# An attention kernel's opening, weight products and last transposes put in another order

## The chip, the cores and the metric

One core of one Trainium2 chip runs the whole kernel. The metric is the device time of one execution in microseconds (us); the time of a kernel is the median of several executions. Engines are named as in the profile: PE is the TensorE matmul stream and PEld its weight loads, DVE is VectorE, ACT is ScalarE, POOL is GpSimd, SP is SyncE, whose queue issues all DMAs of this kernel.

## What is computed

Two attention layers follow one another on an image `x` of 8 batches, 32 by 32 positions (N = 1024) and C = 256 channels, all in f32. Layer 0 has 4 heads, layer 1 has one with a narrow key of 32.

```python
# layer 0
qkv = jnp.einsum('bnc,cd->bnd', xf, W_qkv)      # q, k, v of 4 heads, 256 each
atten = softmax(jnp.einsum('bihd,bjhd->bijh', q, k) * C ** -0.5, axis=2)
res = jnp.einsum('bijh,bjhd->bihd', atten, v).reshape(B, -1, h * C)
x = jnp.einsum('bnd,dc->bnc', res, W_out) + b_out + xf
# layer 1
f, g, h = x @ Wf + bf, x @ Wg + bg, x @ Wh + bh
x = gamma * softmax(g @ f.T) @ h + x
```

## The kernel before, in words

**Layer 0 is folded.** A head's scores are `x (Wq Wk^T) x^T` and its output is `softmax(..) x (Wv Wout)`. So the kernel first forms, for each head h, two 256 by 256 products out of the weights: `wqk` and `wvo`. `fold_weights(h)` (L286) returns five tasks for it: `turn_q`, `turn_k`, `turn_v` (L291), each of which makes four 128 by 128 transposes on PE into one PSUM tile (`pwq`, `pwk`, `pwv`, L296) and copies the tile out (`wqT`, `wvT`; L174 on DVE for q and v, L176 on ACT for k); then `multiply` (L307) twice, each with four 128 by 256 matmuls (L312) into `pwqk` or `pwvo` and a copy out (L174 on DVE for `wqk`, followed there by four small additions `wt`, L846; L176 on ACT for `wvo`). An f32 matmul stands in the trace as two PE records, an f32 transpose as one.

**Products in seven parts.** Queries, scores and value products are done by a Strassen-like scheme, `seven` (L227): seven block products instead of eight, in three tasks `one`, `two`, `three`. Task `one` fills three PSUM banks x, y and z, ACT copies x out (`e`, L263) and DVE adds y to it (`u`, L257). Task `two` accumulates into x and y again; DVE then forms `v` (L257) out of y. Task `three` accumulates into y and z a last time, so it must wait until `v` has been read from y. The sums of the blocks of the image that this needs (`xs`, L399 on DVE) come from `key_sums`, those of the value side (`xt`, L415) from `value_sums`.

**PSUM.** The tag `psm` has two tiles (L862). Weight transposes, weight products, image transposes (`px`), layer 1's projections (`pm_fg`) and output projections (`po`) all take turns in these two: the third of them waits for the copy out of the first. The products in seven parts have six tiles of their own, `ps`.

**Order.** PE, DVE and ACT run in exactly the order in which the program issues the tasks (`manual_schedule`). Work is laid out in steps; a step is half of the query rows (`blk`) of one head of one batch, or half of a layer 1. In a step, `put(tasks, *places)` gives each task a place between about 0 and 10 and the tasks are issued in the order of places. In a layer 0 step the scores stand at 0, 2, 4, 6, 8, 10: two groups of `one`, `two`, `three`. The value products of the step before and the output projection of the step before that are put in between.

**Opening.** `load_x(0, 2)` issues four DMAs of 256 KB for the first image, then `load_weights(h, tag)` (L183) issues for each head a DMA of 512 KB for its q and k weights, one of 256 KB for v and one of 256 KB for the output weights; then small constants (`load_rest`, L158). Five matmuls on zeros (`pm_idle`, L873) come first on PE. Then the tasks of the opening run: four image transposes (`transpose_rows`, L336, L344: halves k = 0, 1 by channel blocks c = 0, 1), the three weight transposes of head 0 with a block sum in between, its two products, its queries with two weight transposes of head 1 in the middle, and the sums over the queries. The other 13 tasks of `fold_weights` for heads 1 to 3 are put at fractions 1.5, 2.1, 2.7, ... of step 0.

**Where the weights lie.** The weights of heads 0 and 3 take the two tiles of the tag `s`, which later hold scores; those of head 1 one of the four tiles of `rows` (which otherwise hold images), those of head 2 a tile of `v`.

**End.** The last step (L979 on) belongs to layer 1 of batch 6: its products (`pa_l`, L828) stand at 1, 4, 6, 8 and the last output projections of batch 7 at 3 and 7. At 8.1 to 8.4 come the four transposes of the finished rows of batch 7 (`px`, copied by ACT, L347), at 9 to 9.3 the projections f and g for its layer 1 (`pm_fg`, L440; ACT adds the bias, L667, and DVE copies, L668). Then follow the scores of the last layer 1 (`ps_l`, L740) and its products.

Of the kernel before, what the change touches and what calls it, by code (L numbers as in the profile page):

```python
# [16 lines left out]
P = 128  # L17
# [3 lines left out]
def kernel(  # L21
# [51 lines left out]
    nc = tc.nc  # L73
# [4 lines left out]
    CC = C // P  # L78
# [31 lines left out]
    def tile_of(tag, shape, name):  # L110
        return pools[tag].tile(shape, F32, tag=tag, name=name)
# [4 lines left out]
    def load_x(b, parts=1):  # L116
        t = tile_of("rows", [P, NT, C], f"x_{b}")
        n = HT // parts
        for k in range(NBLK):
            for i in range(parts):  # L120
                nc.sync.dma_start(
                    t[:, k * HT + i * n : k * HT + (i + 1) * n, :].rearrange("p t c -> p (t c)"),
                    x_v[b][:, k, ts(i, n * C)],
                )
        rows[b] = t
# [57 lines left out]
    def load_weights(h, tag):  # L183

        nw = CC * 3 * C
        t = tile_of(tag, [P, nw + CC * C], f"w_{h}")
        w = t[:, :nw].rearrange("p (c d) -> p c d", c=CC)
        wo = t[:, nw:].rearrange("p (c d) -> p c d", c=CC)
        for part in (slice(0, 2 * C), slice(2 * C, 3 * C)):
            nc.sync.dma_start(w[:, :, part], wqkv_v[:, :, ts(h, 3 * C)][:, :, part])  # L190
        nc.sync.dma_start(wo, wout_v[:, ts(h, CC), :])
        weights[h] = w, wo

# [90 lines left out]
    def fold_weights(h):  # L286

        wT, hold = [], []
        folded[h] = []

        def turn(i, what):  # L291
            w, _ = weights[h]
            pt = tile_of("psm", [P, NB], f"pw{what}_{h}")
            for d in range(CC):
                for c in range(CC):
                    nc.tensor.transpose(  # L296
                        pt[:, d * C + c * P : d * C + (c + 1) * P],
                        w[:, c, i * C + d * P : i * C + (d + 1) * P],
                        ident,
                    )  # L300
            if i != 1:
                hold.append(tile_of("y", [P, N], f"w{what}T_{h}"))
            t = hold[-1][:, ts(i % 2, NB)]
            copy_on(i, t, pt)
            wT.append(t.rearrange("p (d c) -> p d c", d=CC))

        def multiply(i, what):  # L307
            wqT, wkT, wvT = wT
            pm = tile_of("psm", [P, NB], f"p{what}_{h}")
            for c in range(CC):  # L310
                for d in range(CC):
                    nc.tensor.matmul(  # L312
                        pm[:, ts(c, C)],
                        lhsT=(wqT, wvT)[i][:, d, ts(c, P)],
                        rhs=wkT[:, d, :] if i == 0 else weights[h][1][:, d, :],
                        start=(d == 0),
                        stop=(d == CC - 1),
                    )
            t = const.tile([P, CC, C], F32, tag=f"{what}{h}", name=f"{what}{h}")
            copy_on(i, t.rearrange("p c e -> p (c e)"), pm)  # L320
            folded[h].append(t)
            if i == 0:
                t4 = const.tile([P, 4, P], F32, tag=f"wt{h}", name=f"wt{h}")
                sums = [t4[:, k, :] for k in range(4)]
                blocks = [t[:, c, ts(e, P)] for c in range(CC) for e in range(CC)]
                run(sum_b(sums, *blocks))
                wblocks[h] = b_operands(blocks, sums)

        tasks = [partial(turn, i, what) for i, what in enumerate(("q", "k", "v"))]
        tasks += [partial(multiply, i, what) for i, what in enumerate(("wqk", "wvo"))]  # L330
        return tasks

# [510 lines left out]
    def run(*lists):  # L843
        for l in lists:
            for t in l:
                t()  # L846

    def weave(*lists):
# [15 lines left out]
    fast.enter_context(tc.manual_schedule(  # L864
        engines={mybir.EngineType.PE, mybir.EngineType.DVE, mybir.EngineType.Activation}
    ))
    load_x(0, 2)
    idle = tile_of("rs", [P, P], "idle")
    nc.vector.memset(idle, 0.0)
    ident = identity()  # L870
    pm = tile_of("psm", [P, NB], "pm_idle")
    for _ in range(5):
        nc.tensor.matmul(pm[:, :P], lhsT=idle, rhs=idle, start=True, stop=True)  # L873
    load_weights(0, "s")
    load_weights(1, "rows")
    load_weights(2, "v")
    load_weights(3, "s")
    load_rest()

    def behind(b):  # L880
# [10 lines left out]

    first = steps[0][0]
    queries, qsums = first.queries()
    turn_q, turn_k, turn_v, *multiply = fold_weights(0)
    sums = key_sums(0)
    run(transpose_rows(0, rows, xT_of, 0), [turn_q, turn_k, sums[0], turn_v], sums[1:3])
    fold = fold_weights(1) + fold_weights(2) + fold_weights(3)
    run(multiply, sums[3:], queries[:2], fold[:2], queries[2:], qsums)
    first_sums = value_sums(0)

    def is_l0(s):
# [8 lines left out]
    for i, (a, blk) in enumerate(steps):  # L910
        l0 = isinstance(a, Layer0)
        one, two, nxt = step(i - 1), step(i - 2), step(i + 1)
        places = []

        def put(tasks, *at):
            assert len(tasks) == len(at)
            places.extend(zip(at, range(len(places), len(places) + len(at)), tasks))

        if l0:
            put(a.scores(blk), 0, 2, 4, 6, 8, 10)  # L920
        else:
            tasks, _ = a.scores(blk)
            put(tasks, *((0.5, 2.4) if blk == 0 else (0.5, 2)))
        if is_l0(two):
            u, k = two
            put(u.products_of[k][2:], 1 if l0 else 0)
            put([partial(u.invert, k)], 2.9 if l0 or blk == 1 else 1.9)
            put(u.project(k), *((3, 7) if l0 else (2, 6) if blk == 0 else (3, 7)))
        if is_l0(one):
            u, k = one  # L930
            sums, keys = u.sums(k)
            u.products_of[k] = u.products(k)
            put(sums[:2] + sums[3:], *((2.2, 3.2, 4.2) if l0 else (0.8, 2.2, 4.5)))
            put(sums[2:3], 5.2 if l0 else 5.5)
            put(keys, *((6.2, 8.2) if l0 else (7.6, 9.6)))
            put(u.products_of[k][:2], *((5, 9) if l0 else (4, 7)))
        elif one is not None:
            put(one[0].products(one[1]), *((3, 5, 7, 9) if l0 else (1, 4, 6, 8)))
        if i == 0:
            put(fold[2:], -2, -1, *[1.5 + 0.6 * n for n in range(len(fold) - 4)])  # L940
            put(first_sums[:2], 8.4, 9.4)
        if i == 1:
            put(first_sums[2:], 1.4, 3.4)
            put([partial(nc.vector.tensor_scalar, bh_sb, bh_sb, gamma_sb, None, ALU.mult)], 8.5)

        if is_l0(nxt) and blk == NBLK - 1:
            queries, qsums = nxt[0].queries()
            put(queries, *((2.5, 4.5, 6.5) if not l0 else
                            (1.5, 2.5, 4.5) if is_l0(two) else (0.5, 2.5, 5.5)))
            put(qsums, *((6.7, 6.9, 7.3, 7.6) if not l0 else  # L950
                          (5.4, 6.4, 7.2, 7.4) if is_l0(two) else (6.4, 7.2, 7.3, 7.4)))

        if l0 and a.h == 0 and blk == 0:
            put(residual(a.b), 5.3, 6.3, 7.3, 7.4)
        if l0 and a.h == 0 and blk == 1 and a.b > 0:
            put(value_sums(a.b), 1.4, 2.4, 3.4, 4.4)
        if l0 and a.h == 2 and blk == 0 and a.b + 1 < B:
            load_x(a.b + 1)
        if l0 and a.h == 2 and blk == 1 and a.b + 1 < B:
            moves, squares = turn_rows(a.b + 1, rows, xT_of, 0)  # L960
            put(moves, *range(1, 9))
        if l0 and a.h == HEADS - 1 and blk == 0 and a.b + 1 < B:
            put(squares, 0.4, 1.4, 3.4, 4.4)
            put(key_sums(a.b + 1), 5.4, 6.4, 7.2, 7.4)

        if l0 and a.b > 0 and a.h == behind(a.b) - 1:
            if blk == 0:
                moves, turned = turn_rows(a.b - 1, rows1, x1T_of, 1, step(i + 2)[0].fg_tile)
                put(moves, 0.1, 0.2, 0.3, 0.4)
                put(turned, 5.4, 6.4, 7.2, 7.4)  # L970
            else:
                tasks, moves = nxt[0].queries_apart()
                put(tasks, 1.5)
                put(moves, 1.6, 1.7, 1.8, 1.9)
        if not l0 and blk == 0:
            put(a.values(), 0.9, 1, 3, 5, 8)
        if nxt is None:
            put(transpose_rows(B - 1, rows1, x1T_of, 1), 8.1, 8.2, 8.3, 8.4)
            put(final.queries(), 9, 9.1, 9.3)  # L979
        for _, _, t in sorted(places, key=lambda x: x[:2]):  # L980
            t()

# [142 lines left out]
```

## Time and profile before

| what | value |
|---|---|
| time, median of 4 runs (lowest to highest) | 2341.54 us (2340.53 to 2341.98) |
| the profiled execution's own time | 2341.12 us |
| its span, from the first to the last instruction | 2339.2 us |
| PE busy | 2328.7 us |
| DVE busy | 1482.5 us |
| ACT busy | 522.8 us |
| POOL busy | 211.6 us |
| DMA, mean over the span | 18 GB/s |

The execution took 1.9 us outside the span. In a row of the profile's timeline the columns are: start in us, length in us, engine, source line, operation, out<-in by the program's names, partitions and elements, number of instructions, and in brackets the idle time of the engine before the row and what ended it. Ends of matmuls are modelled, so what PE lost between two groups is read from start to start: from the first group's start to the next one's, less the number of records times the steady distance between records. That distance in this trace is 0.216 us for 128x256, 0.429 us for 128x512, and 0.108 us for an f32 transpose of 128x128.

### The profile page before, as it was taken

To read this page: it belongs to the slowest core of one execution; us is meant where nothing else is said; L and a number is where in the kernel's file an instruction comes from. 1 tells how busy PE (TensorE), PEld (TensorE's weight loads), DVE (VectorE), ACT (ScalarE), POOL (GpSimd) and SP (SyncE) were. 2 spreads that over 40 slices of the span, in tenths; PEclk is the share of its full clock that TensorE was granted. 3 is DMA by queue.
4 is the path that set the end of the run, shared out by engine and by line. 5 is a ranking of instruction groups with operands and counts; after the bars stand their busy time and mean duration, and the time that the engine had idled before them with its cause. 6 is when DMAs were issued, how large, how long until landed. Compare 5 with 4: busy or idle time off the path is not lost.

```text
span 2339.2 us, 26029 instructions
## 1 busy us (share of the span) xinstructions
PE 2328.7 (100%) x10394; PEld 1917.8 (82%) x10394; DVE 1482.5 (63%) x2398; ACT 522.8 (22%) x875; POOL 211.6 (9%) x79
## 2 busy tenths in 40 slices
PE   9999999999999999999999999999999999999999
PEld 7888888788877888788887888878888788888877
DVE  6667775377754767557774577645776457766635
ACT  2222222222221222212222122222222222212222
POOL 0111110011110111101111011110001101100110
PEclk9999999999999999999999999999999999999999
DMA  5000010100101001110011000110001100000100
GB/s 138 1 1 1 1 37 14 34 1 8 30 17 32 1 19 21 19 29 1 19 26 18 23 1 19 30 19 19 1 19 30 20 17 1 1 1 1 30 10 29
DMA packets 170257, 42.94 MB, mean 18 GB/s; under 512 B 158160, under 2 KB 163024, under 8 KB 170128
## 3 DMA queue, kind: packets, MB, share of 16 engines
q1 hardware_dynamic: 170128, 41.20, 8.1%
q8 instruction: 84, 1.38, 0.3%
q14 instruction: 45, 0.37, 0.1%
HBM read 13.37 MB, written 8.52 MB: 9 GB/s over the span
## 4 chain that ended last, share of the span: by engine, by line
PE 99%; DVE 1%; ACT 0%; DMA 0%; issue 0%; SPq 0%; ACTq 0%
PE psy_y L240 14%; PE psy L240 14%; PE psx L240 10%; PE pa_l L828 9%; PE po L631 9%; PE psx_y L240 9%; PE psz_y L240 9%; PE psz L240 9%; PE psy_q L240 4%; PE psx_q L240 2%; PE psz_q L240 2%; PE pr_v_l L460 2%; PE ps_l L740 1%; PE pm_fg L697 1%; PE pwqk L312 0%; PE pwvo L312 0%
## 5 line engine op out<-in xcount | busy, mean ns | idle before, releaser
L587 POOL PARTITION_ALL_REDUCE rb<-rs x64 | 207.0, 3234 | 2047.5 <-DVE rs L585 2020.7
L240 PE MATMUL psx<-q,x0T 128*128 128x256 f32 x1024 | 263.5, 380 | 0.0
L240 PE MATMUL psy<-qs,xs 128*128 128x256 f32 x1024 | 262.9, 379 | 0.0
L240 PE MATMUL psz<-q,xs 128*128 128x256 f32 x1024 | 262.8, 379 | 0.0
L535 ACT ACTIVATE p<-p 128x1024 f32<-128x1024 f32 x128 | 135.3, 1057 | 561.6 <-DVE p L257 561.6
L240 PE MATMUL psy_y<-s,xt 128*128 128x256 f32 x1024 | 242.4, 380 | 0.1
L631 PE MATMUL po<-wvo,y 128*128 128x256 f32 x1024 | 242.0, 379 | 0.0
L240 PE MATMUL psx_y<-p,x 128*128 128x256 f32 x1024 | 241.9, 379 | 0.0
L828 PE MATMUL pa_l<-v_l,s_l 128*128 128x257 f32 x1024 | 231.9, 381 | 0.4 <-DVE v_l L723 0.4
L240 PEld LDWEIGHTS psx<-q,x0T 128*128 128x128 f32 x1024 | 193.9, 190 | 45.4 <-issue 20.7
L631 PEld LDWEIGHTS po<-wvo,y 128*128 128x128 f32 x1024 | 194.5, 190 | 40.0 <-issue 15.1
L828 PEld LDWEIGHTS pa_l<-v_l,s_l 128*128 128x128 f32 x1024 | 193.7, 190 | 36.8 <-issue 10.5
L240 PEld LDWEIGHTS psx_y<-p,x 128*128 128x128 f32 x1024 | 194.6, 190 | 34.1 <-issue 8.6
L240 PEld LDWEIGHTS psy_y<-s,xt 128*128 128x128 f32 x1024 | 191.7, 190 | 31.2 <-issue 2.7
L240 PEld LDWEIGHTS psy<-qs,xs 128*128 128x128 f32 x1024 | 194.5, 190 | 26.8 <-DVE qs L506 0.4
L240 PEld LDWEIGHTS psz<-q,xs 128*128 128x128 f32 x1024 | 194.6, 190 | 26.4
L257 DVE TENSOR_TENSOR u<-psy,e 128x512 f32<-128x512 f32 x128 | 88.5, 692 | 146.4 <-PE psy L240 72.3
L269 ACT ACTIVATE p<-psx 128x512 f32<-128x512 f32 x128 | 76.4, 597 | 410.3 <-PE psx L240 410.2
L257 DVE TENSOR_TENSOR v<-psy,e 128x512 f32<-128x512 f32 x128 | 87.9, 687 | 125.3 <-PE psy L240 125.3
L240 PE MATMUL psy<-qs,x0T 128*128 128x256 f32 x512 | 131.5, 379 | 0.8 <-DVE v L257 0.8
L642 DVE SCALAR_TENSOR_TENSOR x<-po,inverse,x 128x256 f32<-128x256 f32 x256 | 112.0, 479 | 31.4 <-PE po L631 22.7
L263 ACT COPY e<-psx 128x512 f32<-128x512 f32 x128 | 73.9, 577 | 256.1 <-PE psx L240 256.1
(120 smaller groups left out, 2840.9 us busy)
## 6 DMA issues: line engine op xcount, KB each, us to landing
out_dram<-x SPq DMA_DIRECT2D x15, 512.0 KB, 2.6
x<-in_x_dram SPq DMA_DIRECT2D x14, 512.0 KB, 4.6
x0T<-x SPq DMA_DIRECT2D x224, 32.0 KB, 1.9
fg<-x SPq DMA_DIRECT2D x112, 64.0 KB, 2.1
fg<-fg SPq DMA_DIRECT2D x56, 64.0 KB, 2.0
w<-in_L_conv_W_qkv_dram SPq DMA_DIRECT2D x4, 512.0 KB, 7.4
x<-in_x_dram SPq DMA_DIRECT2D x4, 256.0 KB, 4.0
w<-in_L_conv_W_qkv_dram SPq DMA_DIRECT2D x4, 256.0 KB, 6.8
```

Of the source, the lines that this page charges most:

```text
L240: nc.tensor.matmul(banks[k][:, ts(i, w)], lhsT=lhsT, rhs=rhs, start=first and n == 0, stop=True, skip_group_check=True,)
L257: nc.vector.tensor_tensor(dst, shaped(banks[k]), shaped(other), ALU.add)
L263: nc.scalar.copy(scratch("e"), banks["x"])
L269: copy(outs["11"](), shaped(banks["x"]))
L460: nc.tensor.matmul(pm[:, ts(j, C)], lhsT=src()[:, c, ts(2 * t2 + j, P)], rhs=w()[:, c, :], start=(c == 0), stop=(c == CC - 1),)
L535: exp(both, both)
L587: nc.gpsimd.partition_all_reduce(t, r.rearrange("p e i -> p (e i)"), P, bass_isa.ReduceOp.add)
L631: nc.tensor.matmul(pm[:, ts(j, C)], lhsT=self.y[blk][:, c, ts(2 * t2 + j, P)], rhs=folded[self.h][1][:, c, :], start=(c == 0), stop=(c == ...
L642: nc.vector.scalar_tensor_tensor(acc, pm[:, ts(j, C)], inverse[:, n : n + 1], acc, ALU.mult, ALU.add)
L697: nc.tensor.matmul(pm[ts(k, half)], lhsT=w[:, c, :], rhs=x1T_of[b][:, c, ts(k, NB)], start=(c == 0), stop=(c == CC - 1),)
L740: nc.tensor.matmul(pm, lhsT=self.f[ts(r, CK), ts(j0 + r, P)], rhs=self.g[ts(r, CK), ts(blk, NB)], start=True, stop=True,)
L828: nc.tensor.matmul(pm[:, : C + 1], lhsT=p[:, j, ts(ti, P)], rhs=v[:, j, : C + 1], start=(j == 0), stop=(j == NT - 1),)
```

## The change

- **Opening, DMA.** `load_weights` issues only on request: it returns two tasks, one for q and k and one for v and the output weights. Head 0's q and k weights are issued ahead of the image, its v and output weights behind it.
- **Opening, order of tasks.** The q and k weights of head 0 are transposed first, then half 0 of the image, then the product `wqk`, then half 1 of the image, then the v weights, two block sums, the product `wvo`, the other two block sums, and the queries as before.
- **Tiles.** Head 3's weights take a tile of `rows` instead of `s`.
- **Heads 1 to 3.** Head 1's remaining three tasks and head 2's five are put in step 0 at -2, -1, 0.5, 1.5, 2.5, 4.5, 6.5, 8.5; head 3's five in step 1 at 0.5, 2.6, 3.5, 5.5, 7.5.
- **End.** In the last step the products stand at 1, 4, 7.2, 8.5; the transposes of batch 7 at 2.5, 4.5, 8.1, 8.2; the f and g projections at 2.4 (which only names tiles), 6.5 and 9.
- `multiply` names the transposed weights by their place in a list instead of unpacking the list first.

```diff
         weights[h] = w, wo
+        v = wqkv_v[:, :, ts(h, 3 * C)]
+
+        def load_qk():
+            nc.sync.dma_start(w[:, :, : 2 * C], v[:, :, : 2 * C])
+
+        def load_v():
+            nc.sync.dma_start(w[:, :, 2 * C :], v[:, :, 2 * C :])
+            nc.sync.dma_start(wo, wout_v[:, ts(h, CC), :])
+
+        return [load_qk, load_v]
...
-                        lhsT=(wqT, wvT)[i][:, d, ts(c, P)],
-                        rhs=wkT[:, d, :] if i == 0 else weights[h][1][:, d, :],
+                        lhsT=wT[2 * i][:, d, ts(c, P)],
+                        rhs=wT[1][:, d, :] if i == 0 else weights[h][1][:, d, :],
...
+    load_qk, load_v = load_weights(0, "s")
+    load_qk()
     load_x(0, 2)
+    load_v()
...
-    load_weights(0, "s")
-    load_weights(1, "rows")
-    load_weights(2, "v")
-    load_weights(3, "s")
+    for h, tag in ((1, "rows"), (2, "v"), (3, "rows")):
+        run(load_weights(h, tag))
     load_rest()
...
-    turn_q, turn_k, turn_v, *multiply = fold_weights(0)
-    sums = key_sums(0)
-    run(transpose_rows(0, rows, xT_of, 0), [turn_q, turn_k, sums[0], turn_v], sums[1:3])
-    fold = fold_weights(1) + fold_weights(2) + fold_weights(3)
-    run(multiply, sums[3:], queries[:2], fold[:2], queries[2:], qsums)
+    turn_q, turn_k, turn_v, fold_qk, fold_vo = fold_weights(0)
+    turn_x, sums = transpose_rows(0, rows, xT_of, 0), key_sums(0)
+    fold = [fold_weights(h) for h in range(1, HEADS)]
+    run([turn_q, turn_k], turn_x[:2], [fold_qk], turn_x[2:], [turn_v], sums[:2], [fold_vo])
+    run(sums[2:], queries[:2], fold[0][:2], queries[2:], qsums)
...
-            put(one[0].products(one[1]), *((3, 5, 7, 9) if l0 else (1, 4, 6, 8)))
+            put(one[0].products(one[1]), *((3, 5, 7, 9) if l0 else (1, 4, 6, 8) if nxt else (1, 4, 7.2, 8.5)))
         if i == 0:
-            put(fold[2:], -2, -1, *[1.5 + 0.6 * n for n in range(len(fold) - 4)])
+            put(fold[0][2:] + fold[1], -2, -1, 0.5, 1.5, 2.5, 4.5, 6.5, 8.5)
             put(first_sums[:2], 8.4, 9.4)
         if i == 1:
             put(first_sums[2:], 1.4, 3.4)
+            put(fold[2], 0.5, 2.6, 3.5, 5.5, 7.5)
...
-            put(transpose_rows(B - 1, rows1, x1T_of, 1), 8.1, 8.2, 8.3, 8.4)
-            put(final.queries(), 9, 9.1, 9.3)
+            put(transpose_rows(B - 1, rows1, x1T_of, 1), 2.5, 4.5, 8.1, 8.2)
+            put(final.queries(), 2.4, 6.5, 9)
```

More of the change, by code (lines that the diff above doesn't have):

```diff
@@ L188, in load_weights @@
         wo = t[:, nw:].rearrange("p (c d) -> p c d", c=CC)
-        for part in (slice(0, 2 * C), slice(2 * C, 3 * C)):
-            nc.sync.dma_start(w[:, :, part], wqkv_v[:, :, ts(h, 3 * C)][:, :, part])
-        nc.sync.dma_start(wo, wout_v[:, ts(h, CC), :])
         weights[h] = w, wo
+        v = wqkv_v[:, :, ts(h, 3 * C)]
[5 more added lines that the diff above has]
+        return [load_qk, load_v]
     def sum_a(sums, a11, a12, a21, a22):
@@ L307, in multiply @@
         def multiply(i, what):
-            wqT, wkT, wvT = wT
             pm = tile_of("psm", [P, NB], f"p{what}_{h}")
```

## The prediction

> **What bounds the kernel now.** I read the page's busy times and chain first, then what PE waited for, then the timeline at both ends.
>
> ```profile
> PE 2328.7 (100%) x10394; PEld 1917.8 (82%) x10394; DVE 1482.5 (63%) x2398; ACT 522.8 (22%) x875; POOL 211.6 (9%) x79
> PE 99%; DVE 1%; ACT 0%; DMA 0%; issue 0%; SPq 0%; ACTq 0%
> ```
>
> PE is the bound from end to end. The change neither adds nor removes PE work (as many transposes and matmuls of each kind; the built order shows the same 3,456 rows), so it can only win what PE loses in waits or at a low clock. What PE waited for in the first 60 us:
>
> ```profile
> PE psy L240 <- DVE v L257: 0.8, 1, 0.8
> PE pwk L296 <- ACT wvo L176: 0.8, 1, 0.8
> PE pwv L296 <- ACT wqT L176: 0.7, 1, 0.7
> PE px L344 <- DMA x<-in_x_dram: 0.6, 2, 0.4
> ```
>
> Columns: us in all, times, longest. Three waits of step 0, and little else. Matmul ends are modelled, so I size them from start to start in the PE timeline:
>
> ```profile
> 30.42 0.60 PE L296 MATMUL pwk<-ident,w 128*128 128x128 f32 x4
> 31.74 0.66 PE L296 MATMUL pwv<-ident,w 128*128 128x128 f32 x4 [0.72 <-ACT wqT L176]
> 32.25 1.99 PE L312 MATMUL pwqk<-wqT 128*128 128x256 f32 x8
> 34.08 1.03 PE L240 MATMUL psy<-qs,x0T 128*128 128x256 f32 x4
> ...
> 37.53 0.60 PE L296 MATMUL pwq<-ident,w 128*128 128x128 f32 x4
> 38.89 0.66 PE L296 MATMUL pwk<-ident,w 128*128 128x128 f32 x4 [0.76 <-ACT wvo L176]
> 39.39 1.03 PE L240 MATMUL psx<-q,x0T 128*128 128x256 f32 x4
> ...
> 46.73 1.03 PE L240 MATMUL psy<-qs,xs 128*128 128x256 f32 x4
> 48.55 0.70 PE L240 MATMUL psy<-qs,x0T 128*128 128x256 f32 x2 [0.78 <-DVE v L257]
> ```
>
> Four transposes are worth 0.43 us, so 30.42 to 31.74 loses 0.89; 31.74 to 34.08 loses another 0.18 (restarting after a wait costs 0.1): 1.07 in all. The second place loses 0.93 + 0.07 = 1.00, the third 1.82 - 0.86 = 0.96 plus 0.1 = 1.06. With 0.26 at 62.62, where psy_y waits for DVE's s, steps 0 and 1 lose 3.39 us. The opening and the end, same columns:
>
> ```profile
> 3.95 2.74 PE L344 MATMUL px<-ident,x 128*128 128x128 f32 x10 [0.40 <-DMA x<-in_x_dram]
> 6.85 1.54 PE L344 MATMUL px<-ident,x 128*128 128x128 f32 x6 [0.16 <-DMA x<-in_x_dram]
> 8.27 1.09 PE L296 MATMUL pwq<-ident,w 128*128 128x128 f32 x4
> 9.15 1.06 PE L296 MATMUL pwk<-ident,w 128*128 128x128 f32 x4
> 10.14 0.66 PE L296 MATMUL pwv<-ident,w 128*128 128x128 f32 x4
> ...
> 14.44 1.02 PE L240 MATMUL psx_q<-x0T,wqk 128*128 128x512 f32 x2
> ```
>
> ```profile
> 2273.04 1.04 PE L344 MATMUL px<-ident,x 128*128 128x128 f32 x8
> 2274.32 1.15 PE L344 MATMUL px<-ident,x 128*128 128x128 f32 x8 [0.24 <-ACT x1T L347]
> 2275.65 3.70 PE L440 MATMUL pm_fg<-x1T,wfg_sb 128*128 128x512 f32 x8 [0.18 <-ACT x1T L347]
> 2279.57 1.14 PE L740 MATMUL ps_l<-fg 32*128 32x512 f32 x8 [0.22 <-DVE fg L668]
> ```
>
> Opening: four transposes take 0.88 us at 8.27 but 0.44 from 10.14 on, so PE's clock doubles at about 10.1. Until then PE is nearly always busy, at half speed. End: eight transposes are worth 0.87, so 2273.04 to 2274.32 loses 0.41, the next stretch 0.46, and eight records of 0.429 leave 0.49 lost before ps_l: 1.36 us.
>
> **What the Trainium skill says.** (1) "TensorE: Matmul & The Clock Gate", Part 1 (the HAM clock gate): PE starts at half clock and is released after about 3.4 us of sustained work, judged in a free-running window. The trace agrees in kind: transposes 0.213 us apart up to 9.8, 0.110 from 10.14. (2) "DMA: Bandwidth & Descriptors", Anatomy of one DMA (SWDGE path): about 2.0 us fixed per DMA; SP's queue is the other path, and here the first 256 KB were issued at 0.74 and used at 3.95, and data flowed at 213 to 291 GB/s between 2 and 5 us, at 359 to 387 between 5 and 9. (3) "Perfetto Trace Analysis", Tensor Engine Instruction: ACT and DVE are strict FIFOs; so a copy sits behind whatever was issued before it, as wvo does behind two exponentials (38.27).
>
> **Opening, worked out.** Hand-over times from this trace: PE to a copy 0.2 us after the last record streams (10.00 to 10.25), a copy 0.59 (ACT) or 0.69 (DVE), copy to PE 0.05. SP issues one DMA per 0.46 us. The new first transfer has 512 KB; before, that many bytes of image were usable at 4.64. I take 4.7. Bounds: 4.0 (just over the 3.95 of half as much) and 6.0 (if it shares bandwidth with the image).
> - pwq 4.75 to 5.60, pwk to 6.45 (half clock). px needs pwq's PSUM tile: 5.60 + 0.2 + 0.69 + 0.05, and 0.1 to restart: 6.66. Two px: 8.37. pwqk from 8.48: four of its eight records at 0.43 until 10.1, four at 0.216: 11.1.
> - px of half 1, 0.43, to 11.5; its sibling needs pwqk's tile, copied by DVE: 11.1 + 0.94 = 12.05, a new wait of 0.5. To 12.5; pwv to 12.97.
> - pwvo needs wvT: 12.97 + 0.94 = 13.94 with restart, a new wait of 0.96. Eight records: psx_q at 15.77, against 14.44: **1.33 us later**. DVE's two block sums behind wvT end at 15.3, before psy_q asks at 16.6. The image's last part would land at about 8.1 (where 1.5 MB stood before) and is asked for at 11: hidden.
>
> Bounds: the 4.0 gives psx_q at 15.5, the 6.0 gives 16.4. If the clock rises at 8.2 it is 15.1, if one window later (13.5) 17.1.
>
> **Steps 0 and 1, worked out.** Built order: pwk_2 and pwv_2 now have two score groups (1.72 us) between them, so the wait at 31.74 goes (it needs 0.94). wvo_2's tile is next taken three tasks later: the wait at 38.89 goes. At 48.55 nothing stood between `two` and `three`; now pwk_2 (0.43) does in the first score group and pwvo_2 (1.73) in the second. First: 0.94 - 0.43 = 0.51, with restart 0.6; new, as four fold tasks stood there before. Second: DVE has wqk_2's copy, four wt, two residual additions (0.69 + 1.11 + 1.36) ahead of v, from pwqk_2's end on; PE does 3.45 us of other work meanwhile, leaving about 0.4, 0.5 with restart. Step 1: DVE gets wqT_3 and wvT_3 ahead of the s that was 0.2 late, PE gets pwq_3, pwk_3, pwv_3 (1.3 us): even, so I count 62.62 as gone. Lost now 1.1 instead of 3.39: **2.29 us sooner**. Bounds: 0 (waits only move) and 3.4 (no waits).
>
> **SP's queue.** Image 1's load issued at 22.6; now it waits for head 1's tile, free when pwvo_1 ends (28.0 before, so about 29.4):
>
> ```profile
> 22.60 0.91 SPq L121 DMA_DIRECT2D x<-in_x_dram  x2
> 29.75 20.99 SPq L371 DMA_DIRECT2D x0T<-x  x32
> 80.23 0.30 SPq L591 DMA_DIRECT2D line<-rb  x1
> ```
>
> Behind it stand 32 moves (21 us), then line<-rb at 80. Load, landing and moves end near 56: 24 us of cover, cost nothing. If that cover were gone, DVE's inverse would be late by the overrun. POOL's reductions keep their order.
>
> **End, worked out.** px of half 0 go under po and pa_l (3.47 us each). pm_fg's first two records (0.86) need channel block 0 only and cover the copy of block 1 (0.2 + 0.59 + 0.05 = 0.84): wait 0 to 0.1. px of half 1 are followed by a pa_l, so pm_fg's second half waits for nothing, and fg for the first scores was made 9 us before. Gain 1.36 less 0.1: **1.25 us**; bounds 0.9 and 1.36.
>
> **Sum.** +1.33 - 2.29 - 1.25 = -2.2 us. The profiled execution, 2341.12 (span 2339.2 and 1.9 around it), becomes 2338.9; the median lies 0.42 above it: 2339.3.
>
> **Rivals.**
> - *Clock sooner, waits smaller* (2337.9, chance 0.15): clock up at 8.2 saves 0.7, half of the two waits in step 0 and half of the wait for wvT another 0.7. For: the window is free-running, the new opening has a dense stream from 4.75. Against: no such run is shown.
> - *Clock one window later* (2340.6, 0.15): pwqk and half 1 at half clock, psx_q at 17.1, 1.3 worse. For: PE idles from 3.3 to 4.7 instead of to 3.95. Against: the stream is dense afterwards.
> - *DVE becomes late in step 1* (2342.5, slower, 0.08): three copies and four additions of head 3 (2.07 + 1.11 = 3.2 us) come ahead of s, p and q. If all lie on the path, -2.2 + 3.2 = +1.0; it turns the sign once over 2.2 us are exposed. For: psy_y already waited for s. Against: DVE is busy 25.0 of the 35 us from 50 to 85.
> - *The order isn't what the text says*: excluded, the built order has it.
>
> **Numbers.** Forecast 0.57, the rivals 0.15, 0.15, 0.08, the rest unknown. Range 2337.8 to 2341.8 takes in both clock cases and the zero bound of step 0 (2341.6). About 0.2% (4.7 us) is what a measurement can tell; no case reaches it: same 0.91, faster 0.05, slower 0.04 for what I don't see.
>
> **What would show it.** pwq at 4.75; transposes 0.213 apart until about 10.1; psx_q near 15.8; waits of 0.5 at px and 0.9 at pwvo; in step 0 two waits on v instead of three waits; no PE wait from 50 to 100; none between px and ps_l at the end. Wrong if psx_q is before 14.4 or after 17.1, or if a wait over 1 us stands in step 1.

## The result, and the profile after

The changed kernel takes 2338.79 us (median; 2338.05 to 2339.95), the kernel before 2341.35 in the same comparison: 2.56 us less, a ratio of 0.999 with a 95% interval of 0.9985 to 0.9994. By the measure of 0.2% (4.7 us) that is no difference, yet the interval leaves 1.0 out. One of the 60 executions of the kernel before took 3509.74 us; the ratio is that of the others. The profiled execution took 2338.24 us (before 2341.12), its span is 2336.4 (before 2339.2).

Busy times and the head of the chain of waits, kernel after:

```profile
PE 2326.8 (100%) x10394; PEld 1917.4 (82%) x10394; DVE 1482.1 (63%) x2398; ACT 522.6 (22%) x875; POOL 211.5 (9%) x79
PE 99%; DVE 1%; DMA 0%; issue 0%; ACT 0%
```

PE has the same 10,394 records and is still the whole chain. What PE waited for in the whole run, longest sums first (us in all, times, longest):

```profile
PE pwq L303 <- DMA w<-in_L_conv_W_qkv_dram: 1.3, 1, 1.3
...
PE pwvo L318 <- ACT x0T L353: 0.8, 1, 0.8
PE psy L247 <- DVE v L264: 0.7, 2, 0.3
...
PE px L350 <- DVE wqk L174: 0.3, 1, 0.3
```

Three waits of 0.7 to 0.8 us (on `wqT`, `wvo` and `v`) became two of 0.3 on `v` by this view, and the opening has two that were not there, at `px` and `pwvo`. From start to start they cost more than the view says. The PE timeline of the opening, after:

```profile
4.82 1.08 PE L303 MATMUL pwq<-ident,w 128*128 128x128 f32 x4 [1.26 <-DMA w<-in_L_conv_W_qkv_dram]
...
6.69 1.97 PE L350 MATMUL px<-ident,x 128*128 128x128 f32 x8
8.48 2.15 PE L318 MATMUL pwqk<-wqT 128*128 128x256 f32 x8
10.46 0.60 PE L350 MATMUL px<-ident,x 128*128 128x128 f32 x4
11.41 0.66 PE L350 MATMUL px<-ident,x 128*128 128x128 f32 x4 [0.35 <-DVE wqk L174]
11.90 0.60 PE L303 MATMUL pwv<-ident,w 128*128 128x128 f32 x4
13.33 1.97 PE L318 MATMUL pwvo<-w,wvT 128*128 128x256 f32 x8 [0.83 <-ACT x0T L353]
15.13 1.02 PE L247 MATMUL psx_q<-x0T,wqk 128*128 128x512 f32 x2
```

`psx_q` starts at 15.13, 0.69 later than the 14.44 of before. Up to `pwqk` the starts are the predicted ones within 0.1 us. `pwqk` then needs 1.98 us to the next start where eight records at half clock would need 3.4: the trace's record of the granted clock turns to full at 8.82, in the kernel before at 10.10. From `px` at 10.46 to its sibling 0.52 of 0.95 us are lost (four transposes are worth 0.43), and 1.00 us ahead of `pwvo`. The bracket there names ACT's copy `x0T`, a wait for several semaphores put down to the wrong one: that copy had ended at 12.68. DVE's timeline, same kernel, shows what was really late:

```profile
10.66 0.69 DVE L174 COPY wqk<-pwqk 128x512 f32<-128x512 f32 x1 [4.03 <-PE pwqk L318]
11.38 0.49 DVE L852 TENSOR_TENSOR wt<-wqk 128x128 f32<-128x128 f32 x2
11.91 0.62 DVE L852 TENSOR_TENSOR wt<-wqk,wt 128x128 f32<-128x128 f32 x2
12.54 0.69 DVE L174 COPY wvT<-pwv 128x512 f32<-128x512 f32 x1
```

`wvT` ends at 13.23 and `pwvo` starts at 13.33. The PE timeline of step 0 and then of the end, after:

```profile
31.11 0.60 PE L303 MATMUL pwk<-ident,w 128*128 128x128 f32 x4
32.06 1.13 PE L247 MATMUL psy<-qs,x0T 128*128 128x256 f32 x4 [0.35 <-DVE v L264]
...
40.37 1.89 PE L318 MATMUL pwvo<-w,wvT 128*128 128x256 f32 x8
42.58 1.13 PE L247 MATMUL psy<-qs,x0T 128*128 128x256 f32 x4 [0.32 <-DVE v L264]
...
57.79 1.89 PE L247 MATMUL psy_y<-s,xt 128*128 128x256 f32 x8
```

```profile
2271.01 1.04 PE L350 MATMUL px<-ident,x 128*128 128x128 f32 x8
2271.88 3.63 PE L834 MATMUL pa_l<-v_l,s_l 128*128 128x257 f32 x16
2275.35 1.88 PE L446 MATMUL pm_fg<-x1T,wfg_sb 128*128 128x512 f32 x4
2277.16 1.14 PE L746 MATMUL ps_l<-fg 32*128 32x512 f32 x8
```

In step 0 the two waits on `v` lose 0.52 and 0.48 (0.95 less four transposes' 0.43; 2.21 less eight records' 1.73), each with 0.1 for the restart; those at 31.74, 38.89 and 48.55 of before are gone. At the end no row from `px` to `ps_l` has a bracket, and `ps_l` starts 2.41 us earlier than the 2279.57 of before. So in these two traces: opening +0.69, end -1.21 (the last step's first `ps_l` is 1.20 earlier, the one behind `pm_fg` 2.41), and what lies between, steps 0 and 1, -1.89.

SP's queue, after:

```profile
29.14 0.81 SPq L121 DMA_DIRECT2D x<-in_x_dram  x2
34.13 21.86 SPq L377 DMA_DIRECT2D x0T<-x  x32
77.31 0.30 SPq L597 DMA_DIRECT2D line<-rb  x1
```

Image 1 is asked for at 29.14 instead of 22.60 and its moves end at 56.0; `line<-rb` is not later but 2.9 us earlier.

### The profile page after: what moved, and what is told of

Same layout as the page of the kernel before. It is cut to its first block, busy times and chain, and to the rows that moved or that the text cites. A ratio compares the mean times of both kernels' runs of the same rounds, so it can differ in the third digit from the quotient of the medians.

```text
span 2336.4 us, 26026 instructions
## 1 busy us (share of the span) xinstructions
PE 2326.8 (100%) x10394; PEld 1917.4 (82%) x10394; DVE 1482.1 (63%) x2398; ACT 522.6 (22%) x875; POOL 211.5 (9%) x79
## 4 chain that ended last, share of the span: by engine, by line
PE 99%; DVE 1%; DMA 0%; issue 0%; ACT 0%
PE psy_y L247 14%; PE psy L247 14%; PE psx L247 9%; PE pa_l L834 9%; PE po L637 9%; PE psz L247 9%; PE psx_y L247 9%; PE psz_y L247 9%; PE psy_q L247 4%; PE psx_q L247 2%; PE psz_q L247 2%; PE pr_v_l L466 2%; PE ps_l L746 1%; PE pm_fg L703 1%; PE pwqk L318 0%; PE pwvo L318 0%
```

## The experiments

Three comparisons, each with its own runs of the kernel before: its median was 2340.96 (opening alone to old opening), 2341.13 (nine idle matmuls to no waits on v) and 2341.38 us (the last three); the row "after" is the comparison above. No kernel leaves out any part of the computation. "psx_q starts" is the end of the opening, and "clock" is when the trace's record of the granted clock turns to full; both are of the one profiled execution.

| kernel | median us | against before | ratio, 95% interval | psx_q starts | clock |
|---|---|---|---|---|---|
| before | | | | 14.44 | 10.1 |
| after | 2338.79 | -2.56 | 0.9985 to 0.9994 | 15.13 | 8.8 |
| opening alone | 2342.71 | +1.75 | 0.9998 to 1.0014 | 15.51 | 9.1 |
| spread alone | 2339.36 | -1.60 | 0.9984 to 1.0001 | 14.28 | 9.1 |
| end alone | 2340.16 | -0.80 | 0.9987 to 1.0003 | 13.76 | 8.4 |
| after, old opening | 2337.94 | -3.02 | 0.9980 to 0.9993 | 13.72 | 4.7 |
| after, 9 idle matmuls | 2337.95 | -3.18 | 0.9979 to 0.9992 | 14.76 | 6.3 |
| after, 1 idle matmul | 2338.91 | -2.22 | 0.9983 to 0.9996 | 15.26 | 8.7 |
| v weights first | 2339.16 | -1.97 | 0.9983 to 1.0000 | 15.87 | 10.6 |
| old opening, no waits on v | 2337.35 | -3.78 | 0.9977 to 0.9991 | 16.17 | 12.4 |
| v weights first, wt last | 2338.29 | -3.09 | 0.9981 to 0.9994 | 15.09 | 9.5 |
| all that gained | 2336.74 | -4.64 | 0.9970 to 0.9988 | 14.09 | 4.2 |
| old opening, 7 idle matmuls | 2338.26 | -3.12 | 0.9979 to 0.9992 | 15.55 | 4.4, lost, 11.2 |

An interval is 2.1 to 4.2 us wide, so medians tell parts of 1 us apart badly; for those the trace is read from start to start.

### The three parts alone

My theory was the sum of the prediction: the opening costs, the spread weight products and the end gain. The opening alone undoes the end and the spread:

```diff
-            put(fold[0][2:] + fold[1], -2, -1, 0.5, 1.5, 2.5, 4.5, 6.5, 8.5)
+            put(fold[0][2:] + fold[1] + fold[2], -2, -1, *[1.5 + 0.6 * n for n in range(11)])
...
-            put(fold[2], 0.5, 2.6, 3.5, 5.5, 7.5)
...
-            put(transpose_rows(B - 1, rows1, x1T_of, 1), 2.5, 4.5, 8.1, 8.2)
-            put(final.queries(), 2.4, 6.5, 9)
+            put(transpose_rows(B - 1, rows1, x1T_of, 1), 8.1, 8.2, 8.3, 8.4)
+            put(final.queries(), 9, 9.1, 9.3)
```

(head 3 back in the tag `s`, the products of the last step back at 1, 4, 6, 8).

> The opening alone: DMA order and task order of the opening as in the changed kernel, everything else as before. My theory, that the opening costs time and the gain comes from elsewhere: 0.5 to 1.4 us slower than before, psx_q starting at 15.0 to 15.8 against 14.44, the three waits of step 0 still there. Rival, that loading the query weights first is what makes the kernel faster: 1.5 to 2.6 us faster, psx_q before 13. Rival, that the opening is neutral because the clock rises sooner in it: within 0.3 us.

Measured 2342.71, 1.75 us above before; that is more than the 1.4 expected, but the interval takes in 1.0. The trace: `psx_q` at 15.51, 1.07 later than before's, with both new waits, and all three waits of step 0 back in their places (the middle one at 39.95). The first and the last in the PE timeline, opening alone:

```profile
32.80 0.66 PE L303 MATMUL pwv<-ident,w 128*128 128x128 f32 x4 [0.72 <-ACT wqT L176]
...
49.60 1.13 PE L247 MATMUL psy<-qs,x0T 128*128 128x256 f32 x4 [0.79 <-DVE v L264]
```

So the new opening does nothing for these three.

The spread alone keeps the new places of heads 1 to 3 and head 3's tile, with the old opening and the old end:

```diff
-    load_qk, load_v = load_weights(0, "s")
-    load_qk()
     load_x(0, 2)
-    load_v()
+    run(load_weights(0, "s"))
...
-    run([turn_q, turn_k], turn_x[:2], [fold_qk], turn_x[2:], [turn_v], sums[:2], [fold_vo])
-    run(sums[2:], queries[:2], fold[0][:2], queries[2:], qsums)
+    run(turn_x, [turn_q, turn_k, sums[0], turn_v], sums[1:3])
+    run([fold_qk, fold_vo], sums[3:], queries[:2], fold[0][:2], queries[2:], qsums)
```

> The spread of the weight products of heads 1 to 3 alone (with head 3's weights in the other tile), opening and end as before. My theory: the three waits of step 0 give way to two waits on v of 0.5 to 0.6 us each, 1.9 to 2.3 us faster than before. Rival, that waits only move to step 1: within 0.4 us of before, with waits of 2 us in all between 49 and 100 us.

Measured -1.60 us, less than the 1.9 expected, with an interval that takes in 1.0. In the trace step 0 has the two waits on `v` (0.51 at 31.20, 0.48 at 41.73) and none of the three old ones; the end has the old waits. One of each in the PE timeline, spread alone:

```profile
31.20 1.13 PE L247 MATMUL psy<-qs,x0T 128*128 128x256 f32 x4 [0.35 <-DVE v L264]
...
2272.27 1.15 PE L350 MATMUL px<-ident,x 128*128 128x128 f32 x8 [0.24 <-ACT x1T L353]
```

The end alone puts only the last step's places into the kernel before:

```diff
-            put(one[0].products(one[1]), *((3, 5, 7, 9) if l0 else (1, 4, 6, 8)))
+            put(one[0].products(one[1]), *((3, 5, 7, 9) if l0 else (1, 4, 6, 8) if nxt else (1, 4, 7.2, 8.5)))
...
-            put(transpose_rows(B - 1, rows1, x1T_of, 1), 8.1, 8.2, 8.3, 8.4)
-            put(final.queries(), 9, 9.1, 9.3)
+            put(transpose_rows(B - 1, rows1, x1T_of, 1), 2.5, 4.5, 8.1, 8.2)
+            put(final.queries(), 2.4, 6.5, 9)
```

> The last step alone: transposes, projections and products placed as in the changed kernel, all else as before. My theory: the three waits between px and the first ps_l go, 1.1 to 1.3 us faster. Rival, that the products after them absorb it, as the last product waits for DVE in both kernels: within 0.4 us of before.

Measured -0.80 us, not told apart from nothing by its interval; in the trace `px`, `pa_l`, `pm_fg` and `ps_l` follow each other without a wait, as in the kernel after, so the 1.2 us are there.

The fourth is the kernel after with the old opening (the diff of the spread, alone):

> The changed kernel with the opening of before: spread and end together. My theory, if the parts add up: 3.1 to 3.5 us faster than before, so 0.5 to 1.3 us faster than the changed kernel. Rival, that the opening helps: slower than the changed kernel by 0.5 us or more.

Measured -3.02 us, the best of the four: spread and end alone give -1.60 - 0.80 = -2.40, so they add up within what is measured. By medians the new opening costs 0.46 here (-2.56 against -3.02, two comparisons) and 1.75 alone: its sign holds, its size isn't settled by medians. By traces: `psx_q` stands at 15.13, 15.51 and 15.26 with the new opening and five idle matmuls or one; with the old one and five idle matmuls at 14.44, 14.28, 13.76, 13.72 and 16.17. That is 15.30 against 14.47 in the mean, 0.8 us, with the clock rising at about 8.9 in the mean of either group. It is a rough figure: the second group spreads over more than the difference, as the clock rose anywhere from 4.7 to 12.4 in it and the image landed late in some.

The other two parts are settled by the traces. From `psx_q` to the first `po` (in step 1, behind the last weight product) PE does the same 300 records in every kernel, only in another order; here are the ends of that stretch in the kernels before and after (the starts, 14.44 and 15.13, are shown above):

```profile
85.13 1.89 PE L631 MATMUL po<-wvo,y 128*128 128x256 f32 x8
```

```profile
83.93 1.89 PE L637 MATMUL po<-wvo,y 128*128 128x256 f32 x8
```

It takes 70.69 us in the three kernels with the old places of the weight products (before, opening alone, end alone) and 68.79 to 68.80 in all eight with the new ones: the spread is worth 1.89 us, whatever opening stands ahead of it. From that `po` to PE's last record it takes 2248.33 and 2248.34 us with the old end (before, spread alone) and 2247.11 to 2247.13 in eight kernels with the new one: 1.21 us. Three of the thirteen traces stand outside this by another 0.35 us, lost once ahead of a `psy_y` (at 1710.85 with the opening alone, near 650 in the two kernels without waits on `v`); why is open. So beside that only the opening's part varies from one execution to the next.

### Half clock: idle matmuls

Theory: what the new opening pays is half clock, since PE stands idle from 3.3 to 4.8 ahead of the first weights. The changed kernel with nine idle matmuls, and with one:

```diff
-    for _ in range(5):
+    for _ in range(9):
         nc.tensor.matmul(pm[:, :P], lhsT=idle, rhs=idle, start=True, stop=True)
```

> The changed kernel with nine matmuls on zeros ahead of the work instead of five, so that PE does not idle between 3.3 and 4.8 us (the work itself is untouched; the extra four write a tile that nothing reads). If half clock is what the new opening pays for: the clock rises between 4.5 and 8, psx_q starts at 14.3 to 14.9 instead of 15.13, 0.3 to 1.0 us faster than the changed kernel. Rival, that the opening is bound by the first landing and the copies alone: psx_q at 15.0 to 15.3, no difference over 0.2 us.

> The changed kernel with one matmul on zeros ahead of the work instead of five. If the clock only counts a window that is busy throughout, the five did nothing here, since PE idled after them anyway: the rise still comes between 8.2 and 11.6 and the time is that of the changed kernel within 0.4 us. Rival, that they do shorten the warm-up: the rise at 9.5 to 11.6, up to 0.7 us slower.

Nine: 2337.95, with the clock up at 6.3 and `psx_q` at 14.76. One: 2338.91, clock at 8.7, `psx_q` at 15.26, no different from five (2338.79, 8.8, 15.13). So the five did nothing in this opening that shows; the nine, which fill the gap ahead of the weights, brought the clock forward: to 6.3 here and to 4.2 in a second kernel with nine below, where with five or one it rose at 8.7 to 10.6 in five executions. PE timeline with nine:

```profile
5.06 1.09 PE L303 MATMUL pwq<-ident,w 128*128 128x128 f32 x4
...
6.93 1.10 PE L350 MATMUL px<-ident,x 128*128 128x128 f32 x8 [0.23 <-DVE wqT L174]
8.26 1.99 PE L318 MATMUL pwqk<-wqT 128*128 128x256 f32 x8 [0.23 <-ACT x0T L353]
```

The eight `px` take 1.33 us to the next start (8.26) instead of 1.79, although a wait of 0.23 was laid bare at each end of them: at full clock the hand-overs show.

### The wait for wvT

Theory: `pwvo` waits a plain hand-over (0.2, a copy of 0.69, 0.05), so the v weights turned one image block earlier halve the wait. Rival: DVE is busy with `wqk` and the four `wt` additions then, and the wait stays.

```diff
-    run([turn_q, turn_k], turn_x[:2], [fold_qk], turn_x[2:], [turn_v], sums[:2], [fold_vo])
+    run([turn_q, turn_k], turn_x[:2], [fold_qk], turn_x[2:3], [turn_v], turn_x[3:], sums[:2], [fold_vo])
```

> The changed kernel with head 0's v weights transposed before the last image block instead of after it, so that the copy wvT has that block's 0.43 us of PE work in front of pwvo. If that wait is the plain turn-around over a copy: pwvo waits 0.4 to 0.6 instead of 1.0, psx_q 0.4 to 0.5 sooner, 0.4 us faster than the changed kernel. Rival, that DVE is late with wvT because of the additions wt: the wait stays near 1.0.

The rival was right: 2339.16, and the wait ahead of `pwvo` is 0.90 us where it was 1.00. DVE's timeline of this kernel:

```profile
12.75 0.62 DVE L852 TENSOR_TENSOR wt<-wqk,wt 128x128 f32<-128x128 f32 x2
13.29 0.68 DVE L174 COPY wvT<-pwv 128x512 f32<-128x512 f32 x1
```

`pwv` was through at 12.7 but its copy started at 13.29, behind the additions. In the kernel after the two limits fall together (the additions end as `pwv` becomes ready, both near 12.5), so neither showed alone. The same with head 0's additions issued behind the copy:

```diff
-                run(sum_b(sums, *blocks))
+                later = partial(run, sum_b(sums, *blocks))
+                hold_sums.append(later) if h == 0 else later()
...
-    run([turn_q, turn_k], turn_x[:2], [fold_qk], turn_x[2:], [turn_v], sums[:2], [fold_vo])
+    run([turn_q, turn_k], turn_x[:2], [fold_qk], turn_x[2:3], [turn_v], hold_sums, turn_x[3:], sums[:2], [fold_vo])
```

> The changed kernel with the v weights turned before the last image block, as tried before, and head 0's four wt additions put behind the copy of wvT on DVE. Theory (the v weights' copy was late because the wt additions stood ahead of it): wvT is copied 0.4 us sooner than with the v weights moved alone, the wait at pwvo falls from 0.90 to about 0.5 us, and from pwqk to psx_q it takes some 0.4 us less: 2338.8 less 0.4 = 2338.4 us by the first comparison's median. Rival (the sums that psy_q reads are now late, since the four wt additions and two block sums end at about 16): a new wait stands between psx_q and psy_q that eats the gain: 2338.8 or more. By medians 0.4 us lies at the edge of what a comparison shows, so the trace decides.

2338.29 us. Timelines of DVE and of PE, `wt` last:

```profile
12.51 0.69 DVE L174 COPY wvT<-pwv 128x512 f32<-128x512 f32 x1 [0.75 <-PE pwv L305]
13.24 0.49 DVE L855 TENSOR_TENSOR wt<-wqk 128x128 f32<-128x128 f32 x2
```

```profile
10.87 0.60 PE L353 MATMUL px<-ident,x 128*128 128x128 f32 x4
...
12.31 0.60 PE L353 MATMUL px<-ident,x 128*128 128x128 f32 x4
13.26 1.99 PE L320 MATMUL pwvo<-w,wvT 128*128 128x256 f32 x8 [0.35 <-DVE wvT L174]
15.09 1.02 PE L247 MATMUL psx_q<-x0T,wqk 128*128 128x512 f32 x2
```

The wait falls to 0.52 (12.31 to 13.26, less 0.43), and from the third `px` to `psx_q` it takes 4.22 us instead of 4.67 in the kernel after. No wait came at `psy_q`. The 0.45 us are shown by the trace, one execution of each; the medians can't separate them.

### The two waits on v

Theory: in step 0 PE waits for `v` because only four transposes stand between `two` and `three` at the first place, and because two residual additions (L431) stand ahead of `v` on DVE at the second. Made on the kernel after with the old opening:

```diff
-            put(fold[0][2:] + fold[1], -2, -1, 0.5, 1.5, 2.5, 4.5, 6.5, 8.5)
+            put(fold[0][2:] + fold[1], -2, -1, 0.5, 2.4, 2.5, 4.5, 6.5, 8.5)
...
-            put(residual(a.b), 5.3, 6.3, 7.3, 7.4)
+            put(residual(a.b), 5.3, 6.3, *((8.6, 8.7) if a.b == 0 else (7.3, 7.4)))
```

> Spread and end with the opening of before, as in the fourth run, and in addition head 2's two first transposes both between the second and third score task of step 0, and the last two residual additions of batch 0 behind the second one's v. If the two waits left in step 0 are what I hold them for (too little PE work in the first, DVE late by two additions in the second): both fall to 0.1 or less, 1.0 to 1.2 us faster than the fourth run, near 2336.8. Rival, that the waits only move on by one task: within 0.3 us of the fourth run.

2337.35 us (-3.78): by the medians 0.76 better than the old opening alone (-3.02, another comparison), less than the 1.0 expected. In the trace both waits are gone. From `psx_q` to `psy_y` it takes 41.63 us (16.17 to 57.80) where the kernel after takes 42.66 (15.13 to 57.79) and the one with the old opening 42.66 too: 1.03 less. (A `psy_y` lost 0.35 at 651.20 in this execution.) DVE and PE timelines at the second place:

```profile
40.70 0.62 DVE L852 TENSOR_TENSOR wt<-wqk,wt 128x128 f32<-128x128 f32 x2
41.23 0.68 DVE L264 TENSOR_TENSOR v<-psy,e 128x512 f32<-128x512 f32 x1
```

```profile
40.97 1.89 PE L318 MATMUL pwvo<-w,wvT 128*128 128x256 f32 x8
42.69 1.03 PE L247 MATMUL psy<-qs,x0T 128*128 128x256 f32 x4
```

The additions of the residual are behind `v` now: it ends at 41.91, 0.78 before PE starts `psy`, which waits for nothing. In the kernel after it ended at 42.52, and `psy` started at 42.58.

### Everything that gained, and the old opening once more

Nine idle matmuls, `wt` last and the two moves against the waits on `v`, on the changed kernel's opening:

> Everything that gained, on the changed kernel's opening: nine idle matmuls, the v weights turned before the last image block with the wt additions behind wvT, and the two moves that took the waits on v out of step 0. Theory (parts add): the changed kernel's -2.3 us against before, -0.9 for the idle matmuls, -0.4 for the wt additions, -0.8 to -1.0 for the two waits: about 4.5 us below before, 2336.6 us, and faster than the old opening with the two waits gone (3.8 below). Rival (the new opening loses to the old one even so, by the two waits that remain in it): not better than 3.8 below before, 2337.3 or more.

2336.74 us, 4.64 below before, where 4.5 was expected: the parts add. PE timeline:

```profile
5.30 0.63 PE L305 MATMUL pwq<-ident,w 128*128 128x128 f32 x4 [0.47 <-DMA w<-in_L_conv_W_qkv_dram]
14.09 1.02 PE L247 MATMUL psx_q<-x0T,wqk 128*128 128x512 f32 x2
```

Here PE runs at full clock when the weights land (four `pwq` take 0.46 us to the next start). It is the fastest measured, though its interval (0.9970 to 0.9988) overlaps that of the old opening without waits on `v` (0.9977 to 0.9991), so that the new opening is the better one is not shown. The last run asks whether the old opening gains by idle matmuls as well (seven instead of five):

> The changed kernel with before's opening, and seven idle matmuls instead of five. In the old opening PE is idle from 3.3 us to the first image block at 3.7 to 4. Theory (the gap ahead of the first real work delays the clock there too): the clock rises earlier and psx_q comes earlier than with five, up to 0.8 us: 2337.1. Rival (the gap is short there and five are enough; or two more delay the first image block): the same as with five, 3.0 us below before, 2337.9, within 0.4.

2338.26 us, as with five (-3.12 and -3.02): by the medians the rival. The trace shows something else beside it. PE timeline, and the view by stretches with PEclk next to last but two (before the DMA share and GB/s):

```profile
4.89 0.88 PE L350 MATMUL px<-ident,x 128*128 128x128 f32 x6 [0.22 <-DMA x<-in_x_dram]
...
7.96 1.54 PE L350 MATMUL px<-ident,x 128*128 128x128 f32 x6 [1.52 <-DMA x<-in_x_dram]
```

```profile
7.00:8.00 1.00, 0.04 (x1) 0.04 (x1) 0.00 (x0) 0.00 (x0) 0.00 (x0) 0.89 0.89 247
8.00:9.00 1.00, 1.00 (x5) 1.00 (x6) 0.00 (x0) 0.32 (x1) 0.00 (x0) 0.50 1.06 294
...
11.00:12.00 1.00, 0.91 (x7) 0.42 (x5) 0.94 (x3) 0.59 (x1) 0.00 (x0) 0.90 1.08 381
```

The clock was full by 4.9 (six transposes in 0.88), then the second half of the image was 1.5 us late, and the clock fell to half from 7.8 to 11.2: the idle matmuls had done their work, and behind the late transfer it was gone. How often that happens isn't settled by one trace; the 21 times of this kernel scatter over 3.9 us (2336.51 to 2340.45), those of the old opening with five over 2.2. (Ahead of the first change on record the view shows 1.00 although transposes stand 0.213 apart; there the distances tell.)

## Why the prediction was right

2339.3 was forecast, 2338.79 measured: -2.2 and -2.56 us. The mechanisms held; two terms, the clock and steps 0 and 1, were off in size by 0.64 and 0.40 us in opposite directions.

- **First landing and order of the opening: right.** `pwq` at 4.82 (4.75 said), `px` 6.69 (6.66), `pwqk` 8.48 (8.48). That it was so close is in part luck: in the five other executions with this order of DMAs where PE waited for the first weights, they were used at 4.75 to 5.30.
- **Clock: too late in the sum, which cost 0.64 us of `psx_q`.** I carried before's 10.1 over; it rose at 8.82, so `psx_q` came at 15.13, not 15.77. (The bound for a rise at 8.2, 15.1, was itself 0.2 too high: with all eight `pwqk` records 0.216 apart the sum gives 14.9.) The opening cost +0.69 in the trace instead of +1.33. That wasn't a property of the new opening that I missed but a draw: over the profiled executions with the new opening and five idle matmuls or one the rise lies between 8.7 and 10.6, with the old one and five between 4.7 and 12.4. The Trainium skill has the ground for it ("TensorE: Matmul & The Clock Gate", Part 1: the window of 3413 ns is free-running, the number of slow matmuls varies from run to run), and the stretch of half clock just shown, 7.8 to 11.2, is 3.4 us long, in agreement. I cited that part and then used one execution's value for the term.
- **New waits: right.** 0.5 at `px` (0.52 measured), 0.96 at `pwvo` (1.00). That the second had two causes at once (the hand-over and DVE's additions) I didn't see; the two runs with the v weights first show it.
- **Steps 0 and 1: mechanism right, the sum 0.4 too good.** Two waits on `v`, 0.6 and 0.5 with restart, measured 0.62 and 0.59. The step that failed is "even, so I count 62.62 as gone": it is gone, but 0.25 us appear at 65.70, and at the same `psy` in all ten traces with the weight products spread. PE there is due for `psy` and DVE is behind:

```profile
64.42 0.62 DVE L852 TENSOR_TENSOR wt<-wqk,wt 128x128 f32<-128x128 f32 x2
64.96 0.68 DVE L264 TENSOR_TENSOR q<-psy_q,e_q 128x512 f32<-128x512 f32 x1
```

  PE's `psy` starts at 65.70, as the addition into `q`, which reads the bank `y`, ends at 65.64; `wt` of head 3 stands ahead of it. That the one delays the other is read from these rows, no run was made for it. It is the slower rival ("DVE late in step 1") at 0.25 of its 3.2 us. Lost: 0.62 + 0.59 + 0.25 = 1.46 instead of 1.1, so 3.39 - 1.46 = 1.93 won (1.89 between the two traces), not 2.29.
- **SP's queue: right.** The load at 29.1 (29.4 said), moves done at 56.0 (56 said), nothing on PE waits for it.
- **End: right.** -1.21 for -1.25. (The prediction gives `po` 3.47 us as it does `pa_l`; eight records are 1.73. The copies are covered all the same.)
- **From the trace to the median.** The sum of the trace at PE's last record is -2.41 (2333.47 to 2331.06); the two profiled executions differ by 2.88, the medians by 2.56. The rest lies behind PE's last record and in what executions differ by; it stays open.

Of the rivals, "clock sooner, waits smaller" happened by half: the clock was sooner, the waits were not smaller. The trace moved by -2.41, near the sum's -2.2, because a cost 0.64 too high for the opening and a gain 0.40 too high for the steps partly cancel; that part of the nearness is luck.

## What to carry to other kernels

In a timeline of back-to-back matmuls, size a wait from start to start and look at what is queued on the copying engine, not only at the hand-over: a move of PE's work gains nothing while additions stand ahead of the copy (0.90 us left of 1.00), and 0.45 once they go behind it. Idle matmuls ahead of the first transfer gained here where they reached up to a landing at about 5 us (by the medians 0.6 to 1.0 us); those that ended 1.5 us before it were worth nothing, and in the old opening, where the gap was 0.3 to 0.6 us, two more changed nothing by the medians. Read the start of full clock from several executions before putting it into a sum: for one and the same opening it spread over nearly 8 us. And where medians can't part two changes, compare the time between two records with the same work between them: for the spread it came out the same within 0.02 us in eight kernels.

## What the hardware showed

- The clock rose among nothing but f32 transposes in the kernel before (0.213 us apart up to 9.8, 0.110 from 10.14, at 10.1, nearly seven us after the last idle matmul). The Trainium skill has it that full clock doesn't engage for transposes ("TensorE: Matmul & The Clock Gate", Part 4: PE-mode transpose); here transposes ran at full clock, and the measurement decides.
- A gap of 1.5 us in PE's work was followed by half clock for 3.4 us in one execution, and in another, with 1.13 and 0.84 us of idle time ahead of two parts of the image, the clock rose only at 12.4. In a third, full from 4.7 on, it stayed full through waits of 0.40 and 0.63 us.
- With the old opening and five idle matmuls (five executions) the first image part was used at 3.63 to 3.95 us, and PE waited for a later part for 0.2 to 1.1 us; with seven, once for 1.5 us.
